# Thirteen nodes to a set instead of twelve in a sparse two-layer graph attention kernel

## The chip, the cores and the metric

The kernel runs on one core of one Trainium2 chip. The metric is the device time of one execution in microseconds (us).

## The reference

Two graph attention layers over one graph of 2048 nodes, for 8 batches, with 64 channels. The first layer has 4 heads, the second one head over the 4 × 64 concatenated channels.

```python
def _gat_layer(h, mask, b):
    scores = jnp.einsum('...nd,...md->...nm', h, h)
    scores = jnp.where(mask, scores, NEG)
    attn = jax.nn.softmax(scores, axis=-1)
    return jnp.einsum('...nm,...md->...nd', attn, h) + b
B, N, C = x.shape                                  # 8, 2048, 64
mask = graph + jnp.eye(N, dtype=graph.dtype) > 0
h = jnp.einsum('bnc,hdc->bhnd', x, Wh)             # 4 heads of 64
out_h = _gat_layer(h, mask[None, None], bh[None, :, None, :])
z = jax.nn.leaky_relu(cat, negative_slope=0.2)     # cat: the heads side by side
h2 = jnp.einsum('bnk,dk->bnd', z, Wo)
out2 = _gat_layer(h2, mask[None], bo)
z2 = jax.nn.leaky_relu(out2, negative_slope=0.2)
...                                                # layer norm over the 64 channels
x = _layernorm(x + that)                           # and a second one after adding x
```

The adjacency matrix is sparse, and denser at low node numbers: the chance of an edge between two nodes falls with the square root of each node's number.

## The kernel before

**Sets.** The first HUB = 56 nodes (the hub) have many neighbours, and their attention is computed densely against all 2048 nodes. The other 1992 nodes form NS = 166 sets of SET = 12: set s holds nodes 56 + s, 56 + s + 166, and so on, every 166th. For each set the kernel finds the union of its members' neighbours, at most 127 and held in a list of 128 slots, and gathers those 128 rows from DRAM with one indirect DMA. Both layers then work on 128 gathered rows for each set, whatever the set's true union is. (If a union is too long, a flag makes a general path run after this one.)

**Start and hub stage (0 to about 125 us).** `load_x` (L458) brings x in 16 blocks of 128 nodes, two DMAs each (two batch parities); the first four blocks go over ACT's queue, the others over SP's. `hubraw` (L474) are the hub's adjacency rows. `make_powers` (L497) builds, on POOL, constants that encode which member of a set a neighbour belongs to; L510 are VectorE's casts behind it, L563 the hub's own mask. The first transposes of x are px (L532, a helper that records every transpose), and L522 copies the turned weights `whT` on ACT. Then for each block `hub_scores` (L621, masked in L625, exponentials in L628) and the hub's values (L639). In the gaps `load_adj` brings the adjacency in 34 half pieces of S10 = 10 sets each (L706), POOL turns them to 0/1 (L711) and sets the members' own entries (L718), and `pick` finds the lists on VectorE. FIRST = 60 sets are picked at a time: the first round here, the other two inside layer 1.

**Layer 1 (about 133 to 585 us).** One loop, `for i in range(-3, NG + 3)`, over NG = 83 pairs of sets, software-pipelined: an iteration computes the scores of pair i+1 (L858), their mask (`weigh`, L863) and exponentials (`lift`, L870), the values of pair i (L883) with normalisation (L890, L891), turns them back (L900, L907), projects pair i−1 to the heads (L551, with z = leaky of it on ACT, L538), applies the second layer's weights to pair i−2 (`second_maps`, L917), turns pair i−3 into rows (L927) and stores them to `table2` (L934). `columns` (L843) prepares the query side of pair i+4 from `own_rows` (L837), and two transposes per iteration turn the gathered rows of pair i+3 (L532). POOL gathers pair i+5 (L829). Rows of M = 48 columns (12 nodes × 4 heads) are one set's queries. All of `project`, `second_maps`, `second_rows` and `columns` write places of one PSUM tile, `cat`.

From i = 30 on, one iteration loads a tile of the own rows of x (`load_own`, L961, 8 DMAs on SP) and the next adds beta on POOL (`add_beta`, L965) and stores it to `table3` (L966); the buffers xb0 and xb1 alternate. There are NV + 1 = 22 such tiles, eight sets to each but the last two.

**Layer 2 (about 590 us to the end).** 42 units of four sets. POOL gathers their rows from `table2` (L829) into a ring of 36 tiles, LEAD = 9 units ahead; PE turns them (L532), computes scores (L1287) and values (L1317), VectorE and ACT do the masking, softmax and both norms (L1342 to L1384). The norm of two units runs on a tile of 128 x 512; `xr` (L1333) is its tile of `table3`, and 8 DMAs store the result (L1400).

What sets the order: each engine runs its instructions in the order written; POOL and SP too have one queue each. SP's and ACT's DMAs share eight completion slots in turn, so a DMA waits until the one eight before it has landed.

Of the kernel before, what the change touches and what calls it, by code (L numbers as in the profile page):

```python
# [44 lines left out]
HUB = 56  # L45
SET = 12
# [313 lines left out]
def fast_kernel(ctx: ExitStack, tc: tile.TileContext, x, adj, Wh, bh, Wo, bo, gamma, beta, out, flag):  # L360


    nc = tc.nc
# [10 lines left out]
    NS = (N - HUB) // SET  # L374
    NG = NS // 2
# [40 lines left out]
    share = [const.tile([P, n], F32, name=f"share{k}") for k, n in enumerate([HALFN, HALFN, HALFN, 512, 512, 2 * 456])]  # L416
# [24 lines left out]
    es = [early.tile([P, 912], F32, name=f"e{k}") for k in range(2)]  # L441
# [13 lines left out]
    def load_x(i):  # L455
        t = xrow[i]
        for p in range(2):
            (nc.scalar if i < 4 else nc.sync).dma_start(out=t[:, :, 1 + p * D:1 + (p + 1) * D],  # L458
                                in_=x[p::2, i * P:(i + 1) * P, :].rearrange("q n c -> n q c"))
# [13 lines left out]
    for k in range(2):  # L473
        nc.sync.dma_start(out=hubraw[k], in_=adj[0:HUB, k * NCH:(k + 1) * NCH])  # L474
# [18 lines left out]
    def make_powers():  # L493
        nc.gpsimd.memset(powers, 0.0)
        d = powers[:, :126].rearrange("p (g c) -> p g c", g=3)[:, :, :10]
        for k in range(SET):
            nc.gpsimd.affine_select(out=d, in_=d, pattern=[[0, 3], [-1, 10]], base=-10 * k, channel_multiplier=1,  # L497
                                    compare_op=OP.not_equal, fill=float(N << k))
# [6 lines left out]
        for row in (0, 32):  # L505
            nc.gpsimd.memset(adds[row:row + 1], 1.0)
        for h in range(2):
            for row, src in ((0, count[0:1, :n].unsqueeze(2).to_broadcast([1, n, SEG // 2])),
                             (32, count[32:33, h * 4:h * 4 + 4].unsqueeze(1).to_broadcast([1, n, SEG // 2]))):
                nc.vector.tensor_copy(number[row:row + 1, h, :].rearrange("p (q j) -> p q j", q=n), src)  # L510

# [71 lines left out]
    def hub_by_sets(c):  # L583
        k = slice(c * SET // 4, (c + 1) * SET // 4)
        nc.scalar.copy(hubs.rearrange("n (s k) -> n s k", k=SET)[:, :, k],
                       hubm[:, HUB:].rearrange("n (k s) -> n s k", s=NS)[:, :, k])

    def hub_mask_sets():
        pm = two("pms")
        cols = hubs  # L590
        for b in range(NHB):
            s0, ns = hub_sets(b)
            nc.tensor.matmul(pm[:ns * SET, b // 9, b % 9 * HUB:(b % 9 + 1) * HUB], cols[:, s0 * SET:(s0 + ns) * SET], identb[:HUB, :HUB],
                             start=True, stop=True)
        for b0, n in ((0, 9), (9, NHB - 10), (NHB - 1, 1)):
            np_ = hub_sets(b0)[1] * SET
            nc.vector.tensor_scalar(maskt[:np_, b0:b0 + n, :].rearrange("p b n -> p (b n)"),
                                    pm[:np_, b0 // 9, b0 % 9 * HUB:(b0 % 9 + n) * HUB], 0.0, 255.0, OP.is_equal, OP.mult)
# [54 lines left out]
    def hub_later(t, new):  # L653
# [19 lines left out]
        def to_table():  # L673
# [24 lines left out]
    byset = adj[HUB:, :].rearrange("(k s) m -> k s m", s=NS)  # L698

    def load_adj(r, t, m):  # L700
# [5 lines left out]
        nc.sync.dma_start(out=raw[:np_], in_=byset[:, s0:s0 + ns, m * NCH:(m + 1) * NCH])  # L706
# [6 lines left out]
        if m == 1:  # L713

            c0 = (HUB + s0) // 2
            for h in range(2):
                d = a[:np_, h, c0:c0 + NS // 2 * SET].rearrange("p (k c) -> p k c", k=SET)[:, :, :ns // 2]
                nc.gpsimd.affine_select(out=d, in_=d, pattern=[[-ns, SET], [-2, ns // 2]], base=-h,  # L718
                                        channel_multiplier=1, compare_op=OP.not_equal, fill=1.0)

    def powers_of(ns, g):
        return powers[:ns * SET, g * 32:(g + 1) * 32] if ns == S10 else powers6[:ns * SET, g, :]

    last = NS % S10
    powers6 = early.tile([120, 3, 32], BF16, name="powers6")
    if last:
        nc.gpsimd.memset(powers6, 0.0)

    def make_powers6():
        g = in_round[NR - 1] // S10 % 3  # L730
        d = powers6[:last * SET, g, 10 * g:10 * g + last]
        for k in range(SET):
            nc.gpsimd.affine_select(out=d, in_=d, pattern=[[-1, last]], base=-last * k, channel_multiplier=1,
                                    compare_op=OP.not_equal, fill=float(N << k))
# [24 lines left out]
    def pick(r):  # L759
# [28 lines left out]
        runs = [(64 * k, s0 + 30 * k, min(30, n_r - 30 * k)) for k in range((n_r + 29) // 30)]  # L788
# [36 lines left out]

    def gather(table, s, layer, new):
        t = rows[layer, s] = new(f"g{layer}_{s}")
        bound = {} if layer == 2 and s < RING else dict(bounds_check=N - 1, oob_is_err=False)
# [3 lines left out]
    def own_rows(m):  # L832

        w = min(4, NS - 4 * m)
        t = held["x", m] = work.tile([P, 2 * GM], F32, tag="xo", name=f"xo{m}", bufs=2)
        src = xT[:, :, HUB:].rearrange("c q (k s) -> c s q k", s=NS)[:, 4 * m:4 * m + w]
        nc.gpsimd.tensor_copy(t[:, :w * 48].rearrange("c (s q k) -> c s q k", s=w, q=Q), src)  # L837

    def columns(g, cat):

        n = min(4, NS - 4 * (g // 2)) * 48
        for k in range(2):
            nc.tensor.matmul(cat[:, k, 2 * GM:2 * GM + n], gram[:, g % 2 * 2 + k, :], held["x", g // 2][:, :n], start=True, stop=True)  # L843

    def keep_columns(g, cat):
        n = min(4, NS - 4 * (g // 2)) * 48
        if g % 2 == 0:
            held["y", g // 2] = work.tile([P, 2 * GM, H], F32, tag="yg", name=f"y{g // 2}", bufs=2)
        nc.scalar.copy(held["y", g // 2][:, :n, g % 2 * 2:g % 2 * 2 + 2], cat[:, :, 2 * GM:2 * GM + n].rearrange("p a n -> p n a"))  # L849
# [11 lines left out]
    def weigh(g, sp):  # L861
# [3 lines left out]
                                mask[:, 2 * g:2 * g + 2, :].rearrange("p s n -> p (s n)").unsqueeze(1).unsqueeze(1)  # L865
# [6 lines left out]
    OQ = 256  # L872

# [19 lines left out]
    def turned(op):  # L893
        return op.rearrange("a j (k c) -> a (j k) c", k=2)[:, :, 2 * (D + 2):2 * (D + 2) + 112]

    def turn_values(g, op):

        osb = held.pop(("o", g))
        for w in range(4):
            nc.tensor.transpose(turned(op)[:, w, :], osb[:112, w].rearrange("a s c -> a (s c)"), ident[:112, :112])  # L900
# [9 lines left out]
    def second_maps(g, ph):  # L910

        z = held.pop(("z", g))
        for hp in range(HP):
            for p in range(2):
                src = z[:, hp, :, p * 48:(p + 1) * 48].rearrange("k s (w n) -> k s w n", w=4)
# [3 lines left out]
    def keep_own(g, ph):  # L919
# [3 lines left out]
        nc.gpsimd.tensor_copy(own[:, :, 2 * g * SET:2 * (g + 1) * SET].rearrange("c q (j n) -> c j q n", j=2),  # L923
# [5 lines left out]
    def keep_rows(g, pr):  # L929
        r = rowts[g % 4]  # L930
        nc.vector.tensor_tensor(r[:GM, 1:1 + P], pr, bob[:GM].rearrange("n p d -> n (p d)"), OP.add)
        dst = table2[HUB:, :].rearrange("(n s) (q c) -> s q n c", s=NS, q=Q)
        for j in range(2):
            (nc.scalar if j and g >= NG - 2 else nc.sync).dma_start(out=dst[2 * g + j], in_=r[j * 48:(j + 1) * 48])  # L934
# [5 lines left out]
    def nodes(t, v):  # L940

        s0 = 8 * v
        b0 = 2 * (t % 2) + t // 2

        def part(ap, a):
            w = min(4, NS - s0 - 4 * a)
            s = s0 + 4 * a
            return ap[b0::4, HUB:, :].rearrange("f (k s) c -> k f s c", s=NS)[:, :, s:s + w, :].rearrange("k f s c -> k f (s c)"), w
        return part

    def load_own(v):
        t = xbs[v % 2]
# [4 lines left out]
        for k in range(4):  # L957
            for a in range(2):
                src, w = nodes(k, v)(x, a)
                p0 = k * 32 + a * SET  # L960
                nc.sync.dma_start(out=t[p0:p0 + SET].rearrange("p (f w) c -> p f (w c)", f=2)[:, :, :w * D], in_=src)  # L961

    def add_beta(v):
        t = xbs[v % 2]
# [36 lines left out]
    for i in range(NB):  # L1001
# [9 lines left out]
        if i == 9:  # L1011
# [8 lines left out]
            if last:  # L1020
# [527 lines left out]
```

## Time and profile before

| | |
|---|---|
| three runs | 862.82, 864.06, 866.0 us (median 864.06) |
| profiled execution | 860.43 us, span 858.6 us, granted clock 0.970 |
| PE busy | 760.2 us (89%) |
| DVE, ACT, POOL busy | 601.5 (70%), 537.9 (63%), 485.3 (57%) us |
| layer 1 scores, first to last | 132.9 to 572.5 us |
| gathers of layer 2, first to last | 590.67 to 813.70 us |

The profiled execution's time is the span and what lies around it. PE is TensorE's matmuls, PEld its weight loads, DVE is VectorE, ACT ScalarE, POOL GpSimd, SP the engine that issues most DMAs; SPq and ACTq are their DMA queues. A timeline row has the start, the length, the engine, the line, the operation, output and input with their shapes, how many instructions were joined into the row, and in square brackets the engine's idle time before it with what ended that. Matmul ends are modelled and overlap the next row, so the time of a group is taken from its start to the next group's start.

### The profile page before, as it was taken

To read this page: it belongs to the slowest core of one execution; us is meant where nothing else is said; L and a number is where in the kernel's file an instruction comes from. 1 tells how busy PE (TensorE), PEld (TensorE's weight loads), DVE (VectorE), ACT (ScalarE), POOL (GpSimd) and SP (SyncE) were. 2 spreads that over 40 slices of the span, in tenths; PEclk is the share of its full clock that TensorE was granted. 3 is DMA by queue.
4 is the path that set the end of the run, shared out by engine and by line. 5 is a ranking of instruction groups with operands and counts; after the bars stand their busy time and mean duration, and the time that the engine had idled before them with its cause. 6 is when DMAs were issued, how large, how long until landed. Compare 5 with 4: busy or idle time off the path is not lost.

```text
span 858.6 us, 42821 instructions
## 1 busy us (share of the span) xinstructions
PE 760.2 (89%) x18461; PEld 651.4 (76%) x18461; DVE 601.5 (70%) x1368; ACT 537.9 (63%) x1175; POOL 485.3 (57%) x619
## 2 busy tenths in 40 slices
PE   4798788899999999999999999998999899998940
PEld 3575567788888898988998988887887778876730
DVE  4347974688887788886556665564248999997895
ACT  2354545566666666666666666663558889887741
POOL 5444563564454456655665666504777777777700
PEclk9899989999999999999999999999999999999975
DMA  6999652443333344444444444335975666665621
GB/s 124 214 243 268 192 171 53 111 118 89 92 88 89 83 118 134 129 120 129 128 130 120 123 123 117 90 108 146 310 202 170 181 189 193 191 180 166 185 55 34
DMA packets 81791, 122.53 MB, mean 143 GB/s; under 512 B 35568, under 2 KB 51852, under 8 KB 81594
## 3 DMA queue, kind: packets, MB, share of 16 engines
q0 software_dynamic: 26784, 65.84, 28.7%
q1 hardware_dynamic: 50374, 52.71, 21.5%
q8 instruction: 148, 2.42, 1.2%
q10 hardware_dynamic: 4436, 1.15, 0.7%
q14 instruction: 49, 0.40, 0.2%
HBM read 123.91 MB, written 18.48 MB: 166 GB/s over the span
## 4 chain that ended last, share of the span: by engine, by line
PE 61%; DVE 17%; DMA 9%; issue 5%; SPq 3%; ACT 3%; POOL 2%; DVEq 0%; POOLq 0%; ACTq 0%
PE o L883 10%; PE s L858 9%; PE bank L532 8%; PE cat L843 6%; DMA rows<-table,index 5%; PE cat L551 4%; PE o L900 3%; PE cat L917 3%; PE t L532 3%; SPq L1400 3%; PE oh L639 3%; PE cat L927 2%; PE sh L621 2%; DMA out_dram<-y_s 2%; PE o L1317 2%
## 5 line engine op out<-in xcount | busy, mean ns | idle before, releaser
L829 POOL DMA_INDIRECT g<-table,index x166 | 175.6, 1058 | 173.6 <-PE o L883 144.8
L829 POOL DMA_INDIRECT rows<-table,index x166 | 173.7, 1046 | 55.1 <-issue 23.2
L863 DVE TENSOR_TENSOR e<-s,mask 128x768 f32<-128x768 f32 x83 | 79.3, 955 | 73.5 <-PE s L858 70.3
L538 ACT ACTIVATE z<-cat,bhp 128x192 f32<-128x192 f32 x166 | 60.7, 416 | 79.4 <-PE cat L551 79.3
L532 PE MATMUL t<-ident,rows 128*128 128x128 f32 x664 | 93.0, 279 | 11.2 <-DMA rows<-table,index 5.2
L883 PE MATMUL o<-g,e 128*64 128x65 f32 x2656 | 97.9, 225 | 3.9 <-issue 3.8
L532 PE MATMUL bank<-ident,g 128*128 128x128 f32 x664 | 99.5, 273 | 1.4 <-DVE e L1059 1.2
L883 PEld LDWEIGHTS o<-g,e 128*64 128x64 f32 x2656 | 85.4, 138 | 14.6 <-issue 4.8
L858 PEld LDWEIGHTS s<-y,xTg 64*64 64x64 f32 x5312 | 85.2, 135 | 13.8 <-issue 13.8
L858 PE MATMUL s<-y,xTg 64*64 64x48 f32 x5312 | 95.5, 221 | 0.0
L1436 ACT COPY xts<-t 128x512 f32<-128x512 f32 x166 | 88.7, 583 | 8.6 <-PE t L532 7.7
L532 PEld LDWEIGHTS t<-ident,rows 128*128 128x128 f32 x664 | 72.9, 141 | 24.0 <-issue 12.2
L1182 ACT COPY xTg<-bank 128x512 f32<-128x512 f32 x166 | 89.0, 596 | 2.5 <-PE bank L532 2.5
L532 PEld LDWEIGHTS bank<-ident,g 128*128 128x128 f32 x664 | 79.0, 141 | 4.1 <-issue 1.3
L849 ACT COPY y<-cat 128x384 f32<-128x384 f32 (+1 forms) x82 | 41.6, 508 | 64.1 <-PE o L900 34.5
L870 ACT ACTIVATE e<-e,shifts 128x768 f32<-128x768 f32 x83 | 80.1, 965 | 2.0 <-DVE e L863 2.0
L711 POOL TENSOR_SCALAR a<-raw 120x1024 bf16<-120x1024 int32 (+1 forms) x34 | 38.5, 1134 | 65.5 <-DMA raw<-in_adj_dram 50.6
L628 ACT ACTIVATE e<-e,shifts 128x896 f32<-128x896 f32 x32 | 33.4, 1043 | 58.1 <-DVE e L625 47.8
L890 DVE RECIPROCAL rall<-o 64x8 f32<-64x8 f32 x166 | 33.9, 205 | 47.8 <-PE o L883 46.5
L843 PE MATMUL cat<-xo,gram 128*128 128x192 f32 (+1 forms) x328 | 66.6, 326 | 0.0
L891 DVE TENSOR_TENSOR osb<-o,rall 128x512 f32<-128x512 f32 x83 | 57.4, 692 | 2.9
L625 DVE TENSOR_TENSOR e<-sh,maskh 128x896 f32<-128x896 f32 x32 | 34.8, 1087 | 31.6 <-PE sh L621 26.6
(195 smaller groups left out, 1529.8 us busy)
## 6 DMA issues: line engine op xcount, KB each, us to landing
raw<-in_adj_dram SPq DMA_DIRECT2D x32, 480.0 KB
table<-xb SPq DMA_DIRECT2D x22, 256.0 KB
xr_s<-table SPq DMA_DIRECT2D x21, 256.0 KB
table<-x SPq DMA_DIRECT2D x16, 260.0 KB
table<-rowt SPq DMA_DIRECT2D x164, 24.4 KB
xb<-in_x_dram SPq DMA_DIRECT2D x164, 24.0 KB
out_dram<-y_s SPq DMA_DIRECT2D x162, 24.0 KB
x<-in_x_dram SPq DMA_DIRECT2D x24, 128.0 KB
```

The costliest lines, as they stand in the source:

```text
L532: nc.tensor.transpose(tp[:, q * P:(q + 1) * P], rows[:, q, 1:1 + P], ident)
L538: nc.scalar.activation(z[:, hp], cat[:, :, hp * n:(hp + 1) * n], AF.Identity, bias=bhp[:, hp:hp + 1], scale=1.0)
L829: nc.gpsimd.indirect_dma_start(out=t.rearrange("n q c -> n (q c)"), out_offset=None, in_=table, in_offset=bass.IndirectOffsetOnAxis(ap=ind ...
L843: nc.tensor.matmul(cat[:, k, 2 * GM:2 * GM + n], gram[:, g % 2 * 2 + k, :], held["x", g // 2][:, :n], start=True, stop=True)
L849: nc.scalar.copy(held["y", g // 2][:, :n, g % 2 * 2:g % 2 * 2 + 2], cat[:, :, 2 * GM:2 * GM + n].rearrange("p a n -> p n a"))
L858: nc.tensor.matmul(sp[half(r), p, (q * 2 + j) * M:(q * 2 + j + 1) * M], xt[half(p), j, q, half(r)], y[half(p), (j * Q + q) * M:(j * Q + q ...
L863: nc.vector.tensor_tensor(e[:, :16 * M].rearrange("p (a q n) -> p a q n", a=2, q=Q), sp[:, :, :8 * M].rearrange("p a (q n) -> p a q n", q= ...
L870: nc.scalar.activation(e[:, :16 * M], e[:, :16 * M], AF.Exp, bias=shifts[:, 0:1], scale=1.0)
L883: nc.tensor.matmul(op[half(p), j, o0:o0 + K1], e[:, c0:c0 + 64], rw[j][:, q, sums(p)], start=True, stop=True)
L891: nc.vector.tensor_tensor(osb, v[:, :, :, 1:K1], r.unsqueeze(3).to_broadcast([P, 4, 2, D]), OP.mult)
L1182: nc.scalar.copy(t[:, k, :], bank[k])
L1436: nc.scalar.copy(xts[s // 2 % 4][:, s % 2, :], tp)
```

## The change

Sets have thirteen members, and there are 153 of them; the hub of dense nodes is 60 wide for what the array wants, of which 59 are stored (BASE = 59), since 59 + 153 × 13 = 2048. The first member of set s is not node 59 + s but the node 72 further on in the first run of 153 (`ROT`), the other twelve members stay at steps of 153. With that the fixed inputs' longest union is 120 rows (119 before). Layer 1 has 77 pairs, of which the last repeats set 151, and layer 2 has 39 units: set 152 alone first, then 38 of four.

```diff
-HUB = 56
-SET = 12
+HUB = 60
+BASE = 59
+SET = 13
+ROT = 72
...
-    NS = (N - HUB) // SET
-    NG = NS // 2
+    NS = (N - BASE) // SET
+    NG = (NS + 1) // 2
...
-    FIRST = 60
+    S10 = 9
+    FIRST = 6 * S10
...
-            (nc.scalar if i < 4 else nc.sync).dma_start(out=t[:, :, 1 + p * D:1 + (p + 1) * D],
-                                in_=x[p::2, i * P:(i + 1) * P, :].rearrange("q n c -> n q c"))
+            for at, node, n in spans(i * P, P):
+                (nc.scalar if i < 4 else nc.sync).dma_start(out=t[at - i * P:at - i * P + n, :, 1 + p * D:1 + (p + 1) * D],
+                                    in_=x[p::2, node:node + n, :].rearrange("q n c -> n q c"))
...
-        nc.sync.dma_start(out=hubraw[k], in_=adj[0:HUB, k * NCH:(k + 1) * NCH])
+        for at, node, n in spans(k * NCH, NCH):
+            nc.sync.dma_start(out=hubraw[k][:, at - k * NCH:at - k * NCH + n], in_=adj[0:HUB, node:node + n])
...
-            nc.tensor.matmul(cat[:, k, 2 * GM:2 * GM + n], gram[:, g % 2 * 2 + k, :], held["x", g // 2][:, :n], start=True, stop=True)
+            nc.tensor.matmul(cat[:, k, :n], gram[:, g % 2 * 2 + k, :], held["x", g // 2][:, :n], start=True, stop=True)
...
-    xbs = [early.tile([P, 8, D], F32, name=f"xb{k}") for k in range(2)]
+    xbs = [early.tile([P, 8, D], F32, name="xb")]
...
-    sets = [list(range(4 * u, min(4 * u + 4, NS))) for u in range(NU)]
+    sets = [[NS - 1]] + [list(range(4 * u, 4 * u + 4)) for u in range(NU - 1)]
...
-                    queue = nc.sync if v < NV - 1 else (nc.sync, nc.scalar, nc.gpsimd)[(2 * t + a) % 3]
+                queue = nc.sync if v != NV - 2 else (nc.sync, nc.scalar, nc.gpsimd)[k % 3]
```

`spans` is new: it cuts a range of permuted node positions into stretches whose nodes are consecutive in DRAM, at the hub's end, at the rotation's wrap and at the end of the first members.

```python
def spans(p0, n):
    for a, b, shift in ((0, BASE, 0), (BASE, BASE + NS - ROT, ROT), (BASE + NS - ROT, BASE + NS, ROT - NS), (BASE + NS, N, 0)):
        lo, hi = max(a, p0), min(b, p0 + n)
        if lo < hi:
            yield lo, lo + shift, hi - lo
```

The first members of a set no longer lie at the same step as the others, so other accesses are split too. Each half piece of the adjacency is two DMAs (108 rows and 9) and is followed by six selections in place of two at its second half. A tile of own rows, and of the output, is 12 DMAs instead of 8 (twelve members each, and the first members by themselves). The columns of `columns` now lie over the place in `cat` where `project` writes, not beside it. POOL's `make_powers6`, for the last, shorter piece, is gone, since 153 is 17 × 9; `make_powers` has 13 steps and 4 small memsets more on VectorE.

On ACT at the start, before (x_120 is node block 0, x_122 block 1; whT the turned weights):

```order
L411 ACT_TABLE_LOAD
L458 DMA x_120<-in_x_dram 128x4x64 x2
L458 DMA x_122<-in_x_dram 128x4x64 x2
L522 COPY whT<-pw 64x256 x2
L614 COPY xT<-px_260 128x4x128
```

and after:

```order
L435 ACT_TABLE_LOAD
L483 DMA x_120<-in_x_dram 59x4x64
L483 DMA x_120<-in_x_dram 69x4x64
L483 DMA x_120<-in_x_dram 59x4x64
L483 DMA x_120<-in_x_dram 69x4x64
L483 DMA x_122<-in_x_dram 12x4x64
L483 DMA x_122<-in_x_dram 72x4x64
L483 DMA x_122<-in_x_dram 44x4x64
L483 DMA x_122<-in_x_dram 12x4x64
L483 DMA x_122<-in_x_dram 72x4x64
L483 DMA x_122<-in_x_dram 44x4x64
L550 COPY whT<-pw 64x256 x2
```

Block 0 comes in four pieces and block 1 in six, all of them ahead of the two copies of whT.

On SP in the later half of layer 1, two tiles of own rows before (table_99 is `table2`, table_168 `table3`; rowt are the rows that `keep_rows` stores):

```order
L961 DMA xb_166<-in_x_dram 12x2x256 x8
L934 DMA table_99<-rowt_115 4x12x130 x2
L966 DMA table_168<-xb_166 128x512
L934 DMA table_99<-rowt_112 4x12x130 x2
L961 DMA xb_167<-in_x_dram 12x2x256 x8
L934 DMA table_99<-rowt_113 4x12x130 x2
L966 DMA table_168<-xb_167 128x512
```

and after (table_174 is `table3`):

```order
L978 DMA table_99<-rowt_115 4x13x130 x2
L1015 DMA table_174<-xb 128x512
L978 DMA table_99<-rowt_112 4x13x130 x2
L1010 DMA xb<-in_x_dram 12x2x256 x4
L1010 DMA xb<-in_x_dram 2x2x256 x2
L1010 DMA xb<-in_x_dram 12x2x256 x4
L1010 DMA xb<-in_x_dram 2x2x256 x2
L978 DMA table_99<-rowt_113 4x13x130 x2
L1015 DMA table_174<-xb 128x512
```

The loads of a tile are twelve and go into the one xb whose store stands two entries ahead of them; before, they went into the other buffer.

More of the change, by code (lines that the diff above doesn't have):

```diff
@@ L415, in fast_kernel @@
     nc.vector.tensor_copy(identb, ident)
-    share = [const.tile([P, n], F32, name=f"share{k}") for k, n in enumerate([HALFN, HALFN, HALFN, 512, 512, 2 * 456])]
+    share = [const.tile([P, n], F32, name=f"share{k}") for k, n in enumerate([HALFN, HALFN, HALFN, 512, 512, 2 * 488])]
     wnat = share[3][:, :H * C].rearrange("p (h c) -> p h c", h=H)
@@ L440, in fast_kernel @@
     maskt = const.tile([P, NHB, HUB], U8, name="maskt")
-    es = [early.tile([P, 912], F32, name=f"e{k}") for k in range(2)]
+    es = [early.tile([P, 964], F32, name=f"e{k}") for k in range(2)]
     rowts = [early.tile([P, PW], F32, name=f"rowt{k}") for k in range(4)]
@@ L504, in make_powers @@
         nc.gpsimd.iota(count[32:33, :8], [[1, 2], [2, SEG // 2]], base=0, channel_multiplier=0)
-        for row in (0, 32):
+        for row in (0, 32, 64):
             nc.gpsimd.memset(adds[row:row + 1], 1.0)
@@ L510, in make_powers @@
                 nc.vector.tensor_copy(number[row:row + 1, h, :].rearrange("p (q j) -> p q j", q=n), src)
+            for at, node, n_ in spans(BASE, NS):
+                nc.vector.memset(number[64:65, h, (node - h + 1) // 2:(node + n_ - h + 1) // 2], float(at - node))
     def weights():
@@ L585, in hub_by_sets @@
         nc.scalar.copy(hubs.rearrange("n (s k) -> n s k", k=SET)[:, :, k],
-                       hubm[:, HUB:].rearrange("n (k s) -> n s k", s=NS)[:, :, k])
+                       hubm[:, BASE:].rearrange("n (k s) -> n s k", s=NS)[:, :, k])
     def hub_mask_sets():
-        pm = two("pms")
+        pm = [two(f"pms{k}") for k in range(2)]
         cols = hubs
@@ L787, in pick @@
         n_r = in_round[r]
-        runs = [(64 * k, s0 + 30 * k, min(30, n_r - 30 * k)) for k in range((n_r + 29) // 30)]
+        w_r = 3 * S10
+        runs = [(64 * k, s0 + w_r * k, min(w_r, n_r - w_r * k)) for k in range((n_r + w_r - 1) // w_r)]
         def slots():
@@ L824, in fast_kernel, with place, pair @@
     RING = 4 * LEAD
+    def place(s):
+        return (s + 1) % NS
+    def pair(s):
+        return 0 if s == NS - 1 else (s + 2) // 2
     def gather(table, s, layer, new):
         t = rows[layer, s] = new(f"g{layer}_{s}")
-        bound = {} if layer == 2 and s < RING else dict(bounds_check=N - 1, oob_is_err=False)
+        if layer == 1:
+            s = set0(s // 2) + s % 2
+        bound = {} if layer == 2 and place(s) < RING else dict(bounds_check=N - 1, oob_is_err=False)
         nc.gpsimd.indirect_dma_start(out=t.rearrange("n q c -> n (q c)"), out_offset=None, in_=table,
@@ L872, in fast_kernel @@
     OQ = 256
+    RC = 64 + M
     def values(g, op):
@@ L899, in turn_values @@
         for w in range(4):
-            nc.tensor.transpose(turned(op)[:, w, :], osb[:112, w].rearrange("a s c -> a (s c)"), ident[:112, :112])
+            nc.tensor.transpose(turned(op)[:, w, :], osb[:RC, w].rearrange("a s c -> a (s c)"), ident[:RC, :RC])
     def keep_values(g, op):
@@ L956, in load_own @@
             return
[L957 to L961, printed above, removed]
+        for dst, src in nodes(v, x, t):
+            nc.sync.dma_start(out=dst, in_=src)
     def add_beta(v):
-        t = xbs[v % 2]
+        t = xbs[v % len(xbs)]
         nc.gpsimd.tensor_tensor(t, t, bet.unsqueeze(1).to_broadcast([P, 8, D]), OP.add)
@@ L1268, in rows2 @@
     def rows2(name):
-        return rowt2[int(name[3:]) % RING]
+        return rowt2[place(int(name[3:])) % RING]
     def gathers(u):
@@ L1477, in fast_kernel @@
             turn_scores(u + 1)
-            a = (u + 1) % 2
-            if u + 3 == NU and len(sets[NU - 1]) < 4:
-                nc.vector.memset(es2[a][:, :, len(sets[NU - 1]):, SET:2 * SET], 1.0)
+            a = side(u + 1)
             keep_scores(u + 1, a)
```

199 lines of the change are left out of this document (115 added, 84 removed).

## The prediction

> **What bounds the kernel now.** I read the page first (which engine is busy: its first part), then windows over the stages, the timeline of PE in one calm iteration of layer 1, and the groups of one line; after that the start, the gathers and the SP queue row by row in the timeline.
>
> ```profile
> PE 760.2 (89%) x18461; PEld 651.4 (76%) x18461; DVE 601.5 (70%) x1368; ACT 537.9 (63%) x1175; POOL 485.3 (57%) x619
> ```
> ```profile
> 220.00:320.00 100.00, 98.14 (x2633) 88.16 (x2628) 79.73 (x217) 66.84 (x153) 50.67 (x68) 1.00 0.35 93
> 420.00:520.00 100.00, 97.26 (x2651) 88.27 (x2643) 60.29 (x142) 65.91 (x152) 64.35 (x78) 1.00 0.46 126
> 700.00:780.00 80.00, 74.56 (x1897) 63.11 (x1885) 74.44 (x131) 70.29 (x165) 62.32 (x59) 1.00 0.65 185
> ```
> ```profile
> 257.11 1.15 PE L858 MATMUL s<-y,xTg 64*64 64x48 f32 x64
> 258.08 0.53 PE L551 MATMUL cat<-otb,whT 64*64 64x96 f32 x16
> 258.54 1.15 PE L883 MATMUL o<-g,e 128*64 128x65 f32 x32
> 259.52 0.50 PE L917 MATMUL cat<-z,woT 128*64 128x96 f32 x8
> 259.95 0.31 PE L927 MATMUL cat<-ident,own 128*96 128x128 f32 x1
> 260.10 0.82 PE L843 MATMUL cat<-xo,gram 128*128 128x192 f32 x4
> 260.76 0.60 PE L532 MATMUL bank<-ident,g 128*128 128x128 f32 x4
> 261.19 0.55 PE L900 MATMUL o<-ident,osb 112*128 112x112 f32 x4
> 261.58 0.60 PE L532 MATMUL bank<-ident,g 128*128 128x128 f32 x4
> 262.11 0.90 PE L858 MATMUL s<-y,xTg 64*64 64x48 f32 x46
> ```
> ```profile
> L858 PE MATMUL s<-y,xTg x5312: 217/218/255, 132.9 to 572.5; 64*64 64x48 f32 x197
> ```
>
> The columns of the windows are length, then PE, PEld, DVE, ACT and POOL busy with their counts, granted clock, DMA share, GB/s. In layer 1 (132.9 to about 580) PE is busy 98.14 of 100 us: one iteration, two sets, is PE's own 5.00 us (262.11 − 257.11), and no other engine is near it. The 83 iterations start over 132.9 to 572.5, so 82 of them take 439.6 us, 5.36 in the mean: 29.6 us lie in stalls around the picking of lists and the start.
>
> Layer 2 is another matter. Its gathers leave POOL one after the other from the first row below to the last, 166 of them:
>
> ```profile
> 590.67 0.98 POOL L829 DMA_INDIRECT rows<-table,index  x1 [4.75 <-DMA hrows<-table]
> 813.70 1.00 POOL L829 DMA_INDIRECT rows<-table,index  x1 [0.30 <-PE t L532]
> ```
>
> 223.03 us for 165 steps, 1.352 us each: about 1.0 busy and 0.30 that stands before every one whatever it names. PE does eight sets in some 9.6 us in the middle, where VectorE is nearly full (74.44 of 80 in the window 700 to 780); eight gathers take 10.8. So PE and VectorE catch up with POOL before the end, and the end of layer 2 is the last gather plus a tail of 44.9 us (813.70 to 858.6).
>
> **The sum, step by step.** It is made against the profiled execution, 860.43 us; the three runs have a median of 864.06, 3.6 us more, which is added at the end.
>
> *1. Fewer iterations in layer 1.* 83 × 5.00 = 415.0 us becomes 77 iterations (153 sets, the last pair partly twice). Each grows where PE streams columns by 13/12: the project L551 0.46 us (to the next row's start) by 0.038, L917 0.43 by 0.036, L843 0.66 by 0.055, L900 0.39 from 112 to 116 columns by 0.014: +0.143. The scores L858 are 64 matmuls in 0.97 us, 15.2 ns each with 48 columns. The nearest row for what more columns cost is the values of layer 2, with 65 columns:
>
> ```profile
> 718.56 1.11 PE L1317 MATMUL o<-rows,share 128*32 128x65 f32 x64
> 719.61 0.66 PE L1298 MATMUL turned_e<-ident,eT 128*128 128x128 f32 x4
> ```
>
> 64 matmuls in 1.05 us, 16.4 ns each: 17 more columns for 1.2 ns. So 48 columns are not what those 0.97 us are spent on, and four more should cost at most 64 × 1.2 × 4/17 = 0.02 us; if they cost in proportion, 0.081. I take 0. Then 77 × 5.143 = 396.0: **−19.0**, between −12.8 (proportional) and −19.0. The 29.6 us of stalls stay. The columns now overwrite the place of the projection, so L843 must wait for its reader z:
>
> ```profile
> 258.68 0.73 ACT L538 ACTIVATE z<-cat,bhp 128x192 f32<-128x192 f32 x2 [0.93 <-PE cat L551]
> ```
>
> It ends at 259.41, 0.69 us ahead of L843 at 260.10; z grows by a twelfth (0.06). Hidden, cost 0.
>
> *2. Fewer gathers in layer 2.* 13 × 1.352 = **−17.6**. The rows per gather stay 128 at both ends. The lone set goes first and takes nothing from this.
>
> *3. Hub stage.* 60 hub nodes for 56 make the scores L621 240 wide for 224, and the masking L625 960 for 896.
>
> ```profile
> L625 DVE TENSOR_TENSOR e<-sh,maskh 128x896 f32<-128x896 f32 x32 | 34.8, 1087 | 31.6 <-PE sh L621 26.6 <-ACT share L739 2.7 <-ACT e L628 2.2
> 43.08 0.99 PE L621 MATMUL sh<-share,xT 64*64 64x224 f32 x16
> 44.00 0.66 PE L532 MATMUL px<-ident,x 128*128 128x128 f32 x4
> ```
>
> L621 takes 0.92 us (43.08 to 44.00), +0.066; L625 +0.078. Until about 71 us PE sets the pace here, after that VectorE with the list picks: some 16 × 0.066 + 16 × 0.078 = **+2.3**, none of it at the least and 32 × 0.078 = 2.5 at the most. Six selections a piece instead of two are POOL's alone; POOL is at 51 of 100 us in layer 1 and waits for raw data here: 0.
>
> *4. The start.* POOL builds the powers, VectorE casts behind that and reaches the hub's mask and the first transposes (timeline; the third row is ACT's queue, issuing the loads of x for node blocks 0 and 1):
>
> ```profile
> 5.55 3.37 POOL L497 TENSOR_SCALAR_AFFINE_SELECT powers<-powers 120x30 bf16<-120x30 bf16 x12
> 9.52 1.25 POOL L506 MEMSET adds<- 1x32 bf16 x2
> 0.77 4.67 ACTq L458 DMA_DIRECT2D x<-in_x_dram  x4
> 12.25 1.29 DVE L563 TENSOR_SCALAR own<-hubraw 56x1024 bf16<-56x1024 int32 x2
> 15.20 1.12 PE L532 MATMUL px<-ident,x 128*128 128x128 f32 x4 [2.74 <-DVE woT L526]
> ```
>
> A thirteenth selection is 3.37/12 = 0.28 us, and four memsets of some 40 elements join VectorE's casts, each below L506's 1.25/2 = 0.62 us: +0.3 to +2.8; the memsets are tiny, and I take +0.9. Beside this, node blocks 0 and 1 now come in 4 and 6 pieces instead of 2 and 2 on ACT's queue, the first hub rows in 4 instead of 1, and the copies of whT stand behind all ten x pieces. The packets of these x loads, in the first 30 us (q10 is ACT's queue):
>
> ```profile
> q10 hardware_dynamic: 3252, 0.81, 13.6%
> ```
>
> 13.6% of 16 engines × 30 us over 3252 packets of 256 bytes is 20 ns a packet. Block 0 has 1024 of them. Spread evenly over 16 engines they take 1.3 us, as now; all on one engine 20.5, and issued from 0.77 on they would land near 24 (with 2.66 us of landing, from the row in step 5), 8.8 us after 15.20, where the transposes need them. What comes next on the chain of work is an x load that already holds it up:
>
> ```profile
> 19.99 8.80 DMA x<-in_x_dram
> ```
>
> It takes 8.80 us among the adjacency loads, so a shift ahead of it may be lost in it or passed on. The pieces cost from 0 to +8; I take +1.6, nearer the even spread, since 15.20 leaves more than ten us to land in: **+2.5** for the start together.
>
> The Trainium skill, page "DMA: Bandwidth & Descriptors", section "Why a DMA increments its semaphore by 16 and not by 1", speaks against this edit: a transfer goes over the largest number of engines up to 16 that divides the slowest dimension of both sides. Block 0 is cut at node 59, into 59 and 69 rows, which by that rule are one engine and three; 2 × 236 + 2 × 92 packets on the first engine are an estimate of 656 × 20 ns = 13.1 us. By that estimate block 0 lands near 17 us, and with the copies behind the ten pieces the start would cost some +4 and the whole sum come to 840; with even spreading it would be 837. No row of this trace shows how a transfer is spread.
>
> *5. The own rows for the last addition, through one buffer.* Twenty-one tiles go x → xb → add on POOL → table3; xb had two buffers and now one, and a tile has 12 loads instead of 8.
>
> First the store to table3 by its line (count, durations in ns, first and last start), then one tile's steps in the timeline, then landings from the chain of work:
>
> ```profile
> L966 SPq DMA_DIRECT2D table<-xb x22: 354/354/363, 315.7 to 536.5; - x22
> ```
> ```profile
> 412.44 3.35 SPq L961 DMA_DIRECT2D xb<-in_x_dram  x8
> 420.75 0.35 SPq L966 DMA_DIRECT2D table<-xb  x1
> 417.04 1.02 POOL L829 DMA_INDIRECT g<-table,index  x1 [1.88 <-PE o L883]
> 419.44 1.28 POOL L965 TENSOR_TENSOR xb<-xb,bet 128x512 f32<-128x512 f32 x1
> 428.75 0.60 PE L532 MATMUL bank<-ident,g 128*128 128x128 f32 x4
> ```
> ```profile
> 699.50 2.21 DMA out_dram<-y_s
> 707.91 3.39 DMA out_dram<-y_s
> 819.78 2.66 DMA xr_s<-table
> ```
>
> Now a tile's first load must wait until the last tile's store has landed. The ring: 12 issues at 0.42 = 5.0 us, their landing 2.66 (the nearest row, another transfer of a whole such tile), the add 1.28, the store with landing 2.66 (stores land in 2.21 to 3.39 in these rows): less the one issue counted twice, 11.2 us. Two iterations take 10.51 in this stage ((536.5 − 315.7)/21), 10.8 with the growth of step 1, 10.3 in a calm one. So SP falls behind by 0.4 us a tile, 8 over 20 tiles. Behind the wait stand SP's row stores to table2 and, as the add is in order on POOL, the gathers of the next iteration; their cover is the gather of 417.04, whose pair's second bank is turned at 428.75: with a landing of 2.66, some 7 us. Cost 8 − 7, and the stalls don't all fall where the ring is late: **+4**, from 0 to 20 × 0.9 − 7 = 11.
>
> *6. Tail.* The last unit is full now; its values were half a unit:
>
> ```profile
> 827.24 0.89 PE L1317 MATMUL o<-rows,share 128*32 128x65 f32 x32 [0.45 <-DVE share L1306]
> ```
>
> That is one more 0.5 us on values, 0.5 on scores and transposes, and four more output stores at 0.42 on SP, over three queues at the very end. The hub steps between the layers grow from 112 to 120 columns (some 0.5 us). VectorE's closing work has the same width: **+2.5**, 0 to 4.
>
> Sum: −19.0 − 17.6 + 2.3 + 2.5 + 4 + 2.5 = −25.3: 835.1 by the profiled execution, **about 838.5** beside the median.
>
> **Rivals.**
> *One buffer paces layer 1.* If the stage's stalls overlap with the ring's, step 5 costs 11: about 846. For it: POOL and SP are in order. Against it: 7 us of cover, and POOL busy in 64 of 100 us there (window 420 to 520).
> *The start slips by 8.* Block 0's 1024 packets on one or two engines, 20.5 us at 20 ns, and ACT's copies behind them: 5.5 more than in the sum, about 844. For it: ten pieces ahead of whT on ACT. Against it: that stretch ends in the 8.80 us load anyway.
> *Scores grow with their columns.* Step 1 is −12.8: about 845. Against it: the 65-column row.
> *The ring makes it slower.* If the landings in this stage, among the gathers' traffic, are the longest seen, 3.4 us and not 2.66, the ring is 12.7 us, 2.4 over the calm pace: 20 × 2.4 − 7 = 41, the sum −25.3 + 37 = +12, about 876. It turns at a cost of 29 in step 5, a ring of 12.1 us.
> *The change doesn't do what it says:* a list over 127 rows would start the general path after the kernel. The fixed inputs give at most 120, so 0.01.
>
> **How the numbers follow.** The forecast, each step near its value, has 0.57, the paced ring 0.17, the start 0.11, growing scores 0.08, the slow ring 0.06 (half of it near the turning point), the general path 0.01. The predicted time is the first, 838.5. The low end is every doubtful cost at its least (ring 0, tail 0, start +0.9, hub 0: −10.4), 828, less 2 if the stalls of 29.6 us shrink with the iterations by 6/83: 826. The high end takes in the ring's 846 and both it and a slipped start, 851. A measurement of this kernel tells about 0.5%, 4.3 us, from no change: faster 0.92, same 0.03, slower 0.05.
>
> **What would show it.** Layer 1: a calm iteration of 5.1 to 5.2 us, with 64 scores matmuls in 0.97 to 0.99. Layer 2: 153 gathers over 205 us. Stores to table3 about 11.2 us apart, with SP waiting for the one before, and PE waiting for gathered rows if the ring paces. The first transposes at 16 to 18 us. The forecast is wrong if the calm iteration is above 5.2, the table3 stores are over 12 us apart, or the tail after the last gather is over 50 us.

## The result, and the profile after

The changed kernel takes 853.62 us in the median against 863.5 of the kernel before, a ratio of 0.988 (95% interval 0.986 to 0.991). It is faster, as forecast, but by 10 us and not by 25, and the time lies above the range. The profiled execution is at 849.53 us, span 847.7. Set beside the trace of before, stage by stage:

| stretch | before, us | after, us | difference | forecast |
|---|---|---|---|---|
| start to the first scores of layer 1 | 132.9 | 136.2 | +3.3 | +4.8 |
| first to last iteration's scores | 438.7 | 431.5 | −7.2 | −19.0 + 4 |
| from there to layer 2's first gather | 19.1 | 20.1 | +1.0 | 0.5 (in the tail's 2.5) |
| first to last gather | 223.0 | 205.4 | −17.6 | −17.6 |
| last gather to the end | 44.9 | 54.6 | +9.7 | +2 |

The two stretches that were missed are layer 1, by 8 us, and the end, by 8 us.

What came out as forecast first. One calm iteration of layer 1 in the timeline of PE, and the line of the scores with its first and last start:

```profile
331.20 1.15 PE L901 MATMUL s<-y,xTg 64*64 64x52 f32 x64
332.17 0.55 PE L579 MATMUL cat<-otb,whT 64*64 64x104 f32 x16
...
334.26 0.87 PE L886 MATMUL cat<-xo,gram 128*128 128x208 f32 x4
334.97 0.60 PE L560 MATMUL bank<-ident,g 128*128 128x128 f32 x4
...
336.34 0.86 PE L901 MATMUL s<-y,xTg 64*64 64x52 f32 x44
```
```profile
L901 PE MATMUL s<-y,xTg x4928: 203/218/258, 136.2 to 568.6; 64*64 64x52 f32 x198
```

5.14 us (336.34 − 331.20), and the 64 scores matmuls take 0.97 us with 52 columns as with 48. The gathers of layer 2:

```profile
587.75 0.98 POOL L872 DMA_INDIRECT rows<-table,index  x1 [5.47 <-DMA hrows<-table]
793.13 1.42 POOL L872 DMA_INDIRECT rows<-table,index  x1 [0.30 <-PE t L560]
```

152 steps in 205.4 us, 1.351 each as before.

**The start.** ACT and PE in the timeline:

```profile
0.78 20.07 ACTq L483 DMA_DIRECT2D x<-in_x_dram  x10
20.88 0.37 ACT L550 COPY whT<-pw 64x256 f32<-64x256 f32 x1 [18.86 <-DMA x<-in_x_dram]
22.09 1.11 PE L560 MATMUL px<-ident,x 128*128 128x128 f32 x4 [5.28 <-DVE woT L554]
```

The ten pieces of x hold ACT's queue until 20.85, the copies of whT stand behind them, and the first transposes are at 22.09 instead of 15.20. About half of these 6.9 us is made up again ahead of layer 1, which begins 3.3 us later.

**The ring of the one buffer.** One tile in the middle of layer 1: SP's queue, the add on POOL, and what POOL waited for there over 140 us.

```profile
L1015 SPq DMA_DIRECT2D table<-xb x21: 349/352/357, 327.4 to 560.5; - x21
```
```profile
435.58 0.35 SPq L1015 DMA_DIRECT2D table<-xb  x1
435.99 1.24 SPq L978 DMA_DIRECT2D table<-rowt  x2
437.66 6.92 SPq L1010 DMA_DIRECT2D xb<-in_x_dram  x14
...
447.52 0.35 SPq L1015 DMA_DIRECT2D table<-xb  x1
```
```profile
446.22 1.28 POOL L1014 TENSOR_TENSOR xb<-xb,bet 128x512 f32<-128x512 f32 x1 [4.20 <-DMA xb<-in_x_dram]
```
```profile
POOL xb L1014 <- DMA table<-rowt: 26.2, 7, 4.0
POOL xb L1014 <- DMA xb<-in_x_dram: 22.2, 6, 5.2
```

The store to `table3` goes out at 435.58, the next tile's loads begin at 437.66 when it has landed, they take 6.92 us to issue, POOL stands until 446.22 for the last to land, and the next store is at 447.52: 11.94 us. This tile has 14 loads, since the rotation wraps in it; a usual one has 12:

```profile
353.55 5.52 SPq L1010 DMA_DIRECT2D xb<-in_x_dram  x12
```

Over all tiles the ring is 233.1/20 = 11.66 us, where two calm iterations take 10.28. POOL's add (in order, ahead of the next gathers) waits 48 us in the window from 412 to 552. In the program it waits for the loads alone, so the waits that the profile names after the row stores (`table<-rowt`) are waits for loads as well.

**The end.** From VectorE's last result to the end of the span it was 7.8 us; now it is 19.6. VectorE's last result and SP's last stores before:

```profile
850.14 0.69 DVE L1379 TENSOR_TENSOR y_s<-y_s,var_s 128x512 f32<-128x512 f32 x1 [0.61 <-ACT var_s L1370]
```
```profile
843.39 11.29 SPq L1400 DMA_DIRECT2D out_dram<-y_s  x19
```

And after: VectorE's and SP's timeline, what SP waited for, and POOL's last instruction of length, a drain at the line that launches the program (durations in ns: shortest, median, longest of three):

```profile
827.38 0.69 DVE L1433 TENSOR_TENSOR y_s<-y_s,var_s 128x512 f32<-128x512 f32 x1 [0.61 <-ACT var_s L1424]
```
```profile
812.12 5.84 SPq L1453 DMA_DIRECT2D out_dram<-y_s  x12
829.66 0.24 SPq L1513 DMA_DIRECT2D flag<-fl  x1
830.01 13.77 SPq L1453 DMA_DIRECT2D out_dram<-y_s  x28
```
```profile
SPq L1513 <- DMA out_dram<-y_s: 11.6, 1, 11.6
```
```profile
L1596 POOLq DRAIN  x3: 46/103/8647, 838.1 to 847.5; - x3
```

SP stands still for 11.6 us ahead of a store of four bytes, the flag, and 28 stores of results queue behind it; they are issued by 843.8, 3.9 us ahead of the end, as the last of SP's stores was in the kernel before. And POOL, whose four stores were out at 830.7, drains for 8.65 us from 838.1 to 846.8, 0.9 us ahead of the end. In the kernel before that drain took 1.87:

```profile
L1543 POOLq DRAIN  x3: 46/103/1869, 853.9 to 858.4; - x3
```

What the flag waits for is told by the order of the program, with the completion slots (DMAHW) that each DMA waits for. SP around the flag, and the first of ACT's four stores of the last group:

```
SP   L1453 DMA out_dram<-y_s_15106 12x2x256 [waits DMAHW7_49]
SP   L1453 DMA out_dram<-y_s_15106 12x2x256 [waits DMAHW1_49]
SP   L1453 DMA out_dram<-y_s_15106 12x2x256 [waits DMAHW3_49]
SP   L1453 DMA out_dram<-y_s_15106 2x2x256 [waits DMAHW5_49]
SP   L1453 DMA out_dram<-y_s_15106 2x2x256 [waits DMAHW7_49]
SP   L1513 DMA flag<-fl 1x1 [waits DMAHW0_49,DVE_49]
ACT  L1453 DMA out_dram<-y_s_15645 12x2x256 [waits DMAHW4_49,DMAHW0_49,DVE_49]
```

The eight slots are dealt in turn, and between SP's stores of group 15106 the slots 0, 2, 4 and 6 are missing: they were dealt to ACT's stores of the very last group, 15645. So the flag waits for slot 0 until a store has landed that can go out only after VectorE's last instruction, and with it wait the 28 stores behind it, of which 24 belong to groups whose results are ready earlier.

### The profile page after: what moved, and what is told of

It reads as the page before. It is cut to its first block, busy times and chain, and to the rows that moved or that the text cites. A ratio compares the mean times of both kernels' runs of the same rounds, so it can differ in the third digit from the quotient of the medians.

```text
span 847.7 us, 40425 instructions
## 1 busy us (share of the span) xinstructions
PE 733.6 (87%) x17262; PEld 620.2 (73%) x17262; DVE 583.1 (69%) x1311; ACT 518.9 (61%) x1099; POOL 469.5 (55%) x643
## 4 chain that ended last, share of the span: by engine, by line
PE 44%; DMA 16%; DVE 15%; SPq 9%; issue 6%; ACT 4%; POOL 3%; POOLq 0%; ACTq 0%; DVEq 0%
PE o L927 6%; PE s L901 6%; SPq L1010 6%; DMA rows<-table,index 5%; PE bank L560 5%; PE cat L886 4%; DMA xb<-in_x_dram 2%; PE cat L579 2%; PE oh L668 2%; DMA table<-xb 2%; SPq L1453 2%; PE t L560 2%; PE sh L650 2%; PE o L944 2%; PE cat L961 2%
## 5 line engine op out<-in xcount | busy, mean ns | idle before, releaser
L872 POOL DMA_INDIRECT rows<-table,index x153 | 160.5, 1049 | 51.8 <-issue 20.4
L906 DVE TENSOR_TENSOR e<-s,mask 128x832 f32<-128x832 f32 x77 | 78.7, 1022 | 74.5 <-PE s L901 68.2
L566 ACT ACTIVATE z<-cat,bhp 128x208 f32<-128x208 f32 x154 | 58.5, 431 | 79.7 <-PE cat L579 78.8
L901 PE MATMUL s<-y,xTg 64*64 64x52 f32 x4928 | 90.0, 221 | 0.3 <-issue 0.3
L560 PEld LDWEIGHTS t<-ident,rows 128*128 128x128 f32 x612 | 66.5, 141 | 20.8 <-issue 10.3
L892 ACT COPY y<-cat 128x416 f32<-128x416 f32 (+1 forms) x76 | 40.5, 535 | 66.0 <-DVE rowt L975 48.5
L913 ACT ACTIVATE e<-e,shifts 128x832 f32<-128x832 f32 x77 | 78.4, 1018 | 2.0 <-DVE e L906 2.0
L742 POOL TENSOR_SCALAR a<-raw 117x1024 bf16<-117x1024 int32 x34 | 39.2, 1156 | 67.1 <-DMA raw<-in_adj_dram 54.6
L1014 POOL TENSOR_TENSOR xb<-xb,bet 128x512 f32<-128x512 f32 x21 | 27.0, 1283 | 73.2 <-DMA xb<-in_x_dram 38.7
L657 ACT ACTIVATE e<-e,shifts 128x960 f32<-128x960 f32 x32 | 35.1, 1096 | 52.7 <-DVE e L654 50.8
L886 PE MATMUL cat<-xo,gram 128*128 128x208 f32 (+1 forms) x304 | 66.1, 341 | 0.0
```

The costliest lines, as they stand in the source:

```text
L560: nc.tensor.transpose(tp[:, q * P:(q + 1) * P], rows[:, q, 1:1 + P], ident)
L566: nc.scalar.activation(z[:, hp], cat[:, :, hp * n:(hp + 1) * n], AF.Identity, bias=bhp[:, hp:hp + 1], scale=1.0)
L872: nc.gpsimd.indirect_dma_start(out=t.rearrange("n q c -> n (q c)"), out_offset=None, in_=table, in_offset=bass.IndirectOffsetOnAxis(ap=ind ...
L886: nc.tensor.matmul(cat[:, k, :n], gram[:, g % 2 * 2 + k, :], held["x", g // 2][:, :n], start=True, stop=True)
L901: nc.tensor.matmul(sp[half(r), p, (q * 2 + j) * M:(q * 2 + j + 1) * M], xt[half(p), j, q, half(r)], y[half(p), (j * Q + q) * M:(j * Q + q ...
L906: nc.vector.tensor_tensor(e[:, :16 * M].rearrange("p (a q n) -> p a q n", a=2, q=Q), sp[:, :, :8 * M].rearrange("p a (q n) -> p a q n", q= ...
```

## The experiments

Two of the three series (t1 to t8) ran on a chip on which the kernel is slower (the kernel before took 1008 and 1013 us there in the median; of the changed kernel, layer 1 begins at 145.9 us, its scores take some 20 us more, and the gathers of layer 2 are 1.9 us apart); they are read by their own traces and by ratios to the kernel before on the same chip. t9 to t12 ran on one like the first.

**The start: whole loads, and wide pieces.**

```diff
 # t2_x_whole
-            for at, node, n in spans(i * P, P):
+            for at, node, n in [(i * P, i * P, P)]:
 # t3_x_wide_pieces: block 0 cut once more, to 48 + 11 and 64 + 5 rows
+            cut = [(at + o, node + o, m) for at, node, n in spans(i * P, P)
+                   for o, m in ((0, n // 16 * 16), (n // 16 * 16, n % 16)) if m] if i == 0 else spans(i * P, P)
```

> Node blocks 0 and 1 of x come as one load per parity again, without the rotation (the first members then have other nodes' x: the values differ, the work does not). Theory (the pieces cost the start): first transposes at 16 to 16.5 us instead of 22.1, layer 1 begins 3 to 6 us earlier than at 136.2, ratio about 0.983. Rival (the shift is lost in the later x loads among the adjacency): first transposes early, but layer 1 begins within 1 us of 136.2, ratio 0.987 to 0.989.

> Block 0 in pieces of 48, 11, 64 and 5 rows instead of 59 and 69: more DMAs (14 on ACT ahead of the copies of whT instead of 10), but no long piece on few DMA engines. Theory (narrow pieces): block 0 and what shares its engine (hub rows, Wo) land by some 9 us, first transposes at 16.5 to 18 us. Rival (the number of loads and slots ahead of the copies): first transposes at 22 us or later.

First transposes, of whole loads and of wide pieces:

```profile
16.04 1.11 PE L560 MATMUL px<-ident,x 128*128 128x128 f32 x4 [0.81 <-DVE woT L554]
```
```profile
17.52 1.11 PE L562 MATMUL px<-ident,x 128*128 128x128 f32 x4 [2.58 <-DMA x<-in_x_dram]
```

21.7 to 22.5 in the seven other runs that kept the pieces of 59 and 69 rows. Fourteen loads ahead of whT let them begin over 4 us sooner than ten, so the pieces' width is the cost and not their number. Layer 1 begins at 144.1 (whole) and 140.4 us (wide), against 145.7 to 147.4 in the four runs of that chip with the narrow pieces. So with whole loads, where 3 to 6 us were expected, it begins some 2 to 3 us sooner, and later than with wide pieces although its transposes are earlier; the runs don't show why. Ratios 0.975 (0.969 to 0.981) and 0.978 (0.974 to 0.982), control 0.987 (0.981 to 0.992).

**The ring.** The same one buffer, but a tile has three iterations from its load to the next one's:

```diff
-        if 0 <= (i - 30) // 2 <= NV:
-            (add_beta if i % 2 else load_own)((i - 30) // 2)
+        if i >= 8 and (i - 8) // 3 <= NV and (i - 8) % 3 != 1:
+            (add_beta if (i - 8) % 3 else load_own)((i - 8) // 3)
```

> The tiles of own rows are spread over three iterations each, from i = 8 on (load at the first, add at the third), with the one buffer kept. Theory (the ring of load, add and store, 11.7 us in the changed kernel, paces layer 1 from i = 30 on): the iterations after i = 45 are at 5.14 us but for the stalls that the kernel before has too, layer 1 is 9 to 12 us shorter, ratio about 0.976. Rival (the stalls there come from the row stores or the gathers themselves): layer 1 shorter by less than 3 us, ratio 0.985 to 0.988; the loads at the picking stage could even cost a few us.

Scores of layer 1, relaxed and in the control on the same chip (t5):

```profile
L901 PE MATMUL s<-y,xTg x4928: 202/218/258, 145.7 to 586.6; 64*64 64x52 f32 x198
```
```profile
L901 PE MATMUL s<-y,xTg x4928: 202/218/258, 145.9 to 599.2; 64*64 64x52 f32 x198
```

440.9 against 453.3 us: 12.4 us less. One profile each is a weak base, since two profiles of the same layer 1 can differ by 5 us (the changed kernel and t12 below). But over all profiles of that chip the stretch from the first to the last iteration's scores is 452 to 457 us in the five with the tight ring (t1, t2, t3, t5, t6) and 437 to 441 us in the three with the relaxed one (t4, t7, t8). The ratio is 0.966 (0.961 to 0.971), lower than expected: some 20 us below the control, of which layer 1 accounts for 12 to 16, and the rest was not located. The ring held layer 1 up, and the rival falls.

**The control, and the tail without ACT.** t1 puts the last group's stores on SP and POOL, t6 those of the last three groups.

```diff
 # t1_tail_off_act
-                queue = nc.sync if v != NV - 2 else (nc.sync, nc.scalar, nc.gpsimd)[k % 3]
+                queue = nc.sync if v != NV - 2 else (nc.sync, nc.gpsimd)[k % 2]
 # t6_tail_sp_pool
+                queue = nc.sync if v < NV - 4 or v == NV - 1 else (nc.sync, nc.gpsimd)[k % 2 if v != NV - 2 else k % 3 == 2]
```

> The last group's output stores go to SP and POOL, none to ACT. Theory (a completion slot): in the changed kernel SP's flag store waits 11.6 us for a slot that was given to one of ACT's last stores, which goes out only after the last result; 28 stores stand behind it. Then here SP does not stand still before the flag, the last store is issued some 4 us after VectorE's last instruction instead of 15.7 us after it, and the time falls by 11 to 13 us, to about 0.974 of the kernel before (the changed kernel: 0.988). Rival (SP simply has more stores than it can issue): SP's stores end at the same distance from VectorE's end within 3 us, ratio 0.985 or more.

> The changed kernel itself, as the control of this chip for the next three. Ratio 0.985 to 0.991 of the kernel before; first transposes near 22 us, stores to table3 about 11.7 us apart, SP's last store issued some 15.7 us after VectorE's last instruction.

> Only the tail: the stores of the last three groups alternate between SP and POOL, none on ACT. Theory (completion slot, then SP's issue rate): SP's last store within 5 us of VectorE's last instruction instead of 15.7; 10 to 12 us below the control, ratio about 0.976. With only the last group moved off ACT, SP's 30 stores still ended 6.3 us after VectorE, so POOL's help should be worth 1 to 3 us more. Rival (the landing of stores, not their issue, ends the kernel): less than 5 us below the control.

Ratios 0.984 (0.980 to 0.988) for t1, 0.987 for the control and 0.989 (0.984 to 0.995) for t6: no gain. SP's queue in t1 around the flag, and POOL's drain there:

```profile
968.56 0.24 SPq L1513 DMA_DIRECT2D flag<-fl  x1
970.48 14.71 SPq L1453 DMA_DIRECT2D out_dram<-y_s  x30
```
```profile
L1596 POOLq DRAIN  x3: 46/103/8811, 986.9 to 996.3; - x3
```

The slot wait is gone (SP waits 0.6 us for the flag's value) and SP's stores end 7.3 us after VectorE's last result instead of 15.7 (the expectation of t6 has 6.3 for it); the span still ends 18.7 us after it, because POOL drains until 995.7. The first theory, that SP's wait alone was on the path, fell: two ends of about equal length lie side by side, and each hides the removal of the other.

**Three undone.** Wide pieces, relaxed ring and the tail of t1 (t7) or of t6 (t8).

> All three costs undone at once: block 0 in pieces of 48, 11, 64 and 5 rows, the own rows one tile per three iterations from i = 8 on, the last group's stores on SP and POOL. If the costs are separate they add up: start 4 to 5, ring 9 to 12, tail 9: 22 to 26 us below the control, ratio 0.958 to 0.964. Rival (one covers another, above all start and ring, since the early tiles' loads fall into the picking stage): 14 to 18 us, ratio 0.968 or more.

> The same with the stores of the last three groups alternating between SP and POOL: 1 to 3 us below the run with only the last group moved, ratio 0.956 to 0.963. The candidate for the fastest version.

0.970 (0.965 to 0.976) and 0.973 (0.969 to 0.978): less than expected of both, and t8 is not below t7. Both still take 18.5 us and more from VectorE's last result to the end, so the tail gave next to nothing; t7 is 18.7 us below the control, where 13 to 17 had been expected of start and ring.

**POOL's drain.** Its length in all runs so far, to the nanosecond the same in those with the same number of POOL's transfers: 8.647 us with 316 of them (five runs), 8.811 with 318, 9.627 with 328, 82 ns for each; but 1.869 with the 339 of the kernel before. If something is emptied every 105 or so full transfers (at 210 and 316 gathers, say, and small stores count for little), all of these fit. Twelve more transfers of 128 rows then shorten the drain:

```diff
+        if 42 <= i < 54:
+            nc.gpsimd.dma_start(out=gam, in_=gamma.partition_broadcast(P))
```

That is t9; t10 has the change of t1 besides, and t12 has every output store on SP (`queue = nc.sync`) and no such loads.

> The changed kernel with twelve more loads on POOL in layer 1 (gamma into its own tile again, 128 rows each, i = 42 to 53). Theory (POOL's drain at the very end grows by 82 ns with each of POOL's transfers since a point that comes every 105 full transfers: 316 were not yet reached with 312, and were passed with 337 in the kernel before): the drain falls from 8.65 to about 1 us. The time stays within 1 us of the control all the same, since SP's stores behind the completion slot end about then too: from VectorE's last instruction to the end 18.5 to 19.5 us (19.3 and 19.6 without the loads). Rival (the drain comes from the four stores on POOL themselves, or from the number of POOL's transfers): 8.6 us or longer, about 9.6.

> The twelve loads on POOL and the last group's stores on SP and POOL, none on ACT: both ends undone. Theory (the slot wait and POOL's drain lie side by side, so that each hides the other): from VectorE's last instruction to the end about 9 to 11 us instead of 19, ratio 0.975 to 0.980. Rival (a third thing ends the kernel): 17 us or more.

> The last group's stores all on SP, none on ACT or POOL, and no extra loads. Theory: no slot wait; POOL has nothing to do after its last gather, so its drain of some 8.3 us starts when the flag is out, about 8 us before VectorE ends, and is hidden; SP issues 36 stores, which end some 9 to 10 us after VectorE: from VectorE's last instruction to the end 11 to 14 us. Rival (POOL's drain begins only when all else is done): 18 us or more.

The drains of t9, t10 and t12:

```profile
L1598 POOLq DRAIN  x3: 46/103/807, 849.7 to 860.3; - x3
```
```profile
L1598 POOLq DRAIN  x3: 46/103/971, 845.5 to 847.0; - x3
```
```profile
L1596 POOLq DRAIN  x3: 46/103/8321, 830.3 to 846.5; - x3
```

0.81 us with 12 transfers more, and with no store on POOL (312) 8.32, just four times 82 ns below 8.647. From VectorE's last result to the end: 19.6 us in t9 (the drain gone, the slot wait still 11.7 us), 11.9 in t10 (both gone) and 14.3 in t12 (no slot wait, the drain begun at 830.3 and over before SP's 36 stores were out). That is the side-by-side theory in all three. t9 has 328 of POOL's transfers as t6 and t8 have, and a drain of 0.81 us instead of 9.63, so their number alone does not set it. The instruction ahead of the drain (INC_SWDGE_SEM) went the same way, 2.31 us in the changed kernel and 0.37 in t9; against that POOL stands 2.35 us between its stores in the three runs with the loads, which no other run shows.

The times follow less well: 0.995 (0.992 to 0.998), 0.988 (0.984 to 0.992) and 0.985 (0.978 to 0.991). t9 was to stay within 1 us of the changed kernel, and its median of 860.45 us is 6.8 above the 853.62 of the first series (this one has no control of its own). t10 was to be at 0.975 to 0.980, and its 853.26 is no gain although its end is 7.7 us shorter. By both the twelve loads cost some 7 us. Layer 1 took 443.0 us in t9 and 438.3 in t10, against 431.5 and 436.7 in the changed kernel and t12, which have no loads. But in the twelve iterations that carry the loads the scores lose 9.8 and 6.7 us against the calm pace, and 7.4 and 6.8 without loads, so the traces do not show where the loads cost. How much of it is theirs and how much is spread between executions was not separated.

**All four undone.** 

> All four undone: wide pieces of block 0, own rows over three iterations each, the last group's stores on SP and POOL, the twelve POOL loads. 8 to 10 us below the run with three undone (0.970), so 0.960 to 0.964 and the fastest. From VectorE's last instruction to the end 9 to 11 us. Rival: the twelve loads cost in layer 1 what they give at the end, 0.968 or more.

832.71 us against 864.01, ratio 0.965 (0.959 to 0.971): the fastest version, 31 us below the kernel before, and just short of the 0.960 to 0.964 expected. Layer 1 begins at 132.1 us and its scores take 425.0, and the end comes 11.7 us after VectorE's last result:

```profile
815.70 0.69 DVE L1437 TENSOR_TENSOR y_s<-y_s,var_s 128x512 f32<-128x512 f32 x1 [0.61 <-ACT var_s L1428]
```
```profile
808.94 14.95 SPq L1457 DMA_DIRECT2D out_dram<-y_s  x30
```

SP's 30 stores, issued until 7.5 us after VectorE's last result (3.9 in the kernel before), are what is left of it.

## Why the prediction was right or wrong

*Step 1, fewer iterations: right.* 5.14 us a calm iteration, as summed (5.143), and the scores did not grow.

*Step 2, fewer gathers: right.* −17.6 us, to the tenth.

*Step 3 and 4, hub and start: near in size, by luck.* +3.3 by the first scores, against +4.8. The transposes slipped by 6.9 and not by 2.5, and from there to layer 1 the kernel became 3.6 us shorter, where step 3 had made it 2.3 longer: part of the slip was absorbed, as step 4 allowed, and what the hub stage's wider rows cost is hidden in it. The runs t2 and t3 decide what the trace of before could not: the narrow pieces are the cost. The rule of the Trainium skill that the prediction weighed (page "DMA: Bandwidth & Descriptors", section "Why a DMA increments its semaphore by 16 and not by 1") agrees with them: 59 rows are one engine by it, 48 are sixteen, and 14 loads in wide pieces let the transposes begin at 17.5 us where 10 loads in narrow ones let them begin at 21.7 to 22.5. By the prediction's estimate from that rule block 0 lands near 17 us; no row shows that landing by itself, and ACT's queue is free behind all ten pieces at 20.85.

*Step 5, the one buffer: the mechanism was right, the ring was mis-sized.* The step named the ring, its parts and its victims. It put the ring at 11.2 us, and it was 11.66 in the mean (11.0 to 12.9 in the tiles of full length). The term that failed is the issue of the loads: 12 × 0.42 = 5.0 us in the sum, 5.9 in the mean of the first 18 tiles, since the four loads of two first members, for which the trace of before had no row, take 0.50 to 0.58 us each in the usual tile shown above, and the eight of twelve members 0.31 to 0.42. The store with its landing (2.4) and the landing of the loads (2.2) were shorter than the 2.66 taken for each, but the one issue that the sum took off was not saved. So small an error counts twenty times: with 11.66 the step's own formula, 20 × (11.66 − 10.8) − 7, gives 10 us instead of the 1 that the step raised to 4.

PE's iterations bear the formula out. While the stores to table3 run, 40 iterations (331.20 to 557.46) take 20.7 us more than 5.14 each; 41 of the kernel before (319.26 to 535.03) took 11.2 more than 4.99 each. So the ring cost 9.5 us, and 3.5 more were lost ahead of it. In t12, whose layer 1 is the same, the ring is 240.3/20 = 12.0 us, the formula gives 17, and the iterations lose 16.6. The cover of 7 us held in both. The rival "one buffer paces layer 1" named a price of 11, but its reason was another: a ring of 11.2 against the calm pace of 10.3. With the ring as measured that would be 20 us, and 27 in t12. That its price fits is luck.

*Step 6, the tail: wrong, the path was missed.* +2.5 was forecast (2 of it behind the last gather), +9.7 came: the slot wait of 11.6 us on SP and the drain of 8.65 us on POOL, side by side. The step counted four more stores and more work of VectorE, and looked at neither the completion slots across queues, though the order of the program showed them before any run, nor the drain, of which the trace of before has a row of 1.87 us. VectorE's own end came even 2.2 us sooner after the last gather (34.9 against 37.1 us).

*The sum.* Layer 1, above all by step 5, and the end, by step 6, miss by 8 us each, 15 to 16 together; step 3 and 4 give 1.5 back. With all four costs undone the kernel is at 0.965, 31 us below, where the prediction had 25 with a slipped start and a partly paced ring in it.

## What to carry to other kernels

A buffer that is made single closes a ring: sum its period from issue, landing, work and store, and compare it with the pace of the loop. Where the two are close, a few tenths of a microsecond in one part decide (0.46 us in twenty turns were 9 us here), so take each part from a row of its own shape, and give the range the width of that error. Before the last stores are spread over queues, look at which completion slot each was given: a store that waits for the last result can hold a slot that an earlier one on another queue needs. Where taking away a wait that the trace shows brings nothing, look for a second end of the same length beside it, and take both away.

## What the runs showed of the hardware

- POOL's drain at the end of the program took 82 ns for each of its DMAs since some point: 0.81 to 9.63 us here. Twelve DMAs more took 7.8 us off it. That the point comes every 105 or so full transfers fits the seven lengths seen, but what is emptied there was not shown.
- A DMA of four bytes waited 11.6 us for a store of another engine's queue, since in this program both queues share eight completion slots. With no store on that queue the wait was 0.6 us (t1).
- With a load of 128 rows cut into 59 and 69 the first transposes came at 21.7 to 22.5 us, with one cut into 48, 11, 64 and 5 at 17.4 to 17.6, and with a whole one at 16.0.
- Small DMAs issued back to back on SP took 0.31 to 0.42 us each with twelve rows and 0.50 to 0.58 with two (the tile of own rows at 353.55).
